# A graph layer's node-side product kept as three bfloat16 parts, and a comparison's constants kept in the PSUM bank of the counts

## The chip, the core and the metric

The kernel runs on one core of a Trainium2 chip. The metric is the device time of one execution in microseconds (us). Before the change, ten runs gave a median of 2495.02 us (2490.36 to 2504.91). The core has five engines that each work through a queue of their own in order: PE (TensorE, matrix products into PSUM; PEld is its load of the stationary operand), DVE (VectorE), ACT (ScalarE), POOL (GpSimd, which here issues the scattering transfers) and SP (SyncE, which here issues the other transfers). PSUM is the memory that PE writes its results to; it is divided into banks of 2 KB in each of 128 partitions.

## The reference

A layer of a graph network over N = 12,500 nodes of 64 features and E = 212,500 edges (`src`, `dst`, one weight each), sorted by `dst`:

```python
h = jnp.maximum(_layernorm(x, axis=-1), 0.0)
edge_in = jnp.concatenate([h[row], h[col], dist], axis=1)      # row = src, col = dst
e = jax.nn.silu(edge_in @ eW1 + eb1)
e = jax.nn.silu(e @ eW2 + eb2)
agg = jax.ops.segment_sum(e, row, num_segments=h.shape[0])
node_in = jnp.concatenate([h, agg], axis=1)
out = jax.nn.silu(node_in @ nW1 + nb1) @ nW2 + nb2
x = x + out
```

All numbers are float32. Since `edge_in @ eW1` is a sum over its parts, it can be formed as A[src] + B[dst] + dist * w + eb1, with A = h @ eW1[:64] and B = h @ eW1[64:128] computed once for each node.

## The kernel before

**Two tables.** `products` (line 668) computes, for four of the hundred "buckets" of 125 nodes at a time, A into the DRAM table `ta` and B into `tb` (256 KB stores from SP, lines 678 and 683); it runs 25 times. It is a generator: each `yield` is a place at which other work is put between its steps. `turns` (line 687) keeps up to three of these generators going at once, and the iterator `feed` hands out their steps, four or three to a piece of the work below, later two to a hook.

**Sending the edges.** The edges come in 208 blocks of 1024 in order of `dst`. For each block, `count` (line 344) finds for every edge its place in the bucket of its `src`. On DVE it compares the block's bucket numbers `bkE` with the row 1 to 100 of `nodes1` (lines 354 to 359; 128x800 results `oh` in bfloat16), reduces `oh` to counts `each` (line 362), and later multiplies `oh` with the running counts `full` (line 402), reduces that to `rank` (line 404) and makes the row numbers `to` (line 406). The running counts lie in PSUM: PE adds `before` times `each` to them (line 388) and, at the start of the next block's turn, `rest` times `each` (line 347). `send` (line 412) forms B[dst] + dist * w + eb1 for the block's edges with eight matrix products (line 427), copies them to SBUF on ACT (lines 437 and 443), and POOL scatters the rows to the DRAM array `q` in eight indirect transfers for each block (line 450; 1661 in all). The tile `to` has four buffers (line 268), so the `to` of one block waits until the scatters of the block four back have landed. Each block's turn is cut in three pieces (`PIECES`, line 486).

**Working off the rows.** The rows of `q` are taken in twelve levels (`LEVELS`, line 56) of 25 batches of four buckets. Levels 0, 1 and 8 to 11 have one row of 128 slots for each bucket (one step to a batch), levels 2 to 7 have two (two steps to a batch); there are 450 steps of four 128-row tiles. A level is fetched when all blocks that can write to it have been sent. `fetch` (line 492) loads a batch of `q` rows (`qt`) and the four buckets' rows of `ta` (`a`) four batches ahead. A step then is:

- `s_lr`, line 526: PE spreads each row's node number (bfloat16) over 125 partitions;
- `s_one_t`, line 531: DVE compares it, giving the one-hot matrix `oneT`;
- `s_pt`, lines 540 and 546: PE transposes the four tiles into `pt`, and adds `a` times `oneT`, which gives each row its A[src]; one product of 128 columns for each of four tiles where a batch has one step, one of 256 columns for each of two buckets where it has two; then ACT applies SiLU (line 550);
- `s_bias`, `s_p2`, lines 572 to 582: the second layer, float32;
- `s_one`, `s_seg`, `s_add`, lines 559, 592 and 603: another one-hot matrix, and the sums for each node, added to `aggT` on DVE.

In the last level each batch ends with the node layer (`nodes`, line 239). The queues of PE, DVE, ACT and SP are written out in the order of the program: the table `turn` (line 610) lists the parts of a step with the steps they run ahead, and each `None` in it is a hook at which pieces of the sending are put in, at a rate (`marks`) that finishes a level's blocks before that level's first fetch. If a check of the lists' assumptions fails, `general_sums` (line 950) computes all of it in another way; the profile has no instruction of it.

Of the kernel before, what the change touches and what calls it, by code (L numbers as in the profile page):

```python
# [38 lines left out]
P = 128  # L39
L = 125  # L40
# [8 lines left out]
TB = BLK // P  # L49
PAIR = 2 * BLK  # L50
BEYOND = 20
G = 4
# [21 lines left out]
def tile_gnn(ctx: ExitStack, tc: tile.TileContext, x, src, dst, ew, eW1, eb1, eW2, eb2, nW1, nb1, nW2, nb2, out):  # L74
# [111 lines left out]
    bad = const.tile([P, 2], F32, name="bad")  # L186
    nc.vector.memset(bad, 0.0)

    ta = dram.tile([P * NB, H], F32, name="ta")
    tb = dram.tile([P * NB, H], F32, name="tb")  # L190
    dests = dram.tile([NP, NQR, 2, QR], BF16, name="dests")

# [76 lines left out]
    with ExitStack() as work:  # L269
# [5 lines left out]
                engines={mybir.EngineType.PE, mybir.EngineType.DVE, mybir.EngineType.Activation, mybir.EngineType.SP}  # L275
            )
        )
        full = sgp.tile([P, NB], F32, name="full")
        nc.tensor.matmul(full, before, identb[:, :NB], start=True, stop=True)
        nc.vector.memset(full, -1.0)  # L280
        mine = cnt.tile([P, TB, NB], F32, name="mine")
        sums = []
        blk, lists = {}, {}
# [60 lines left out]
        def count(s):  # L344

            if s > 0:
                nc.tensor.matmul(full, rest, sums.pop(), start=False, stop=True, skip_group_check=True)
            if s < nblocks:
                bc, win, pick = blk[s]
                p, g = s // 2, s % 2  # L350
                whole = p > 0 and (2 * p + 2) * BLK <= E
                buckets = bkE[:, g * TB : (g + 1) * TB, p]
                oh = wk.tile([P, TB, NB], BF16, name="oh")
                nc.vector.tensor_tensor(  # L354
                    oh,
                    nodes1[:, None, :NB].to_broadcast([P, TB, NB]),
                    buckets[:, :, None].to_broadcast([P, TB, NB]),
                    op=OP.is_equal,
                )
                each = wk.tile([P, NB], BF16, name="each")  # L360
                with nc.allow_low_precision("whole numbers up to eight"):
                    nc.vector.tensor_reduce(each, oh.rearrange("p t b -> p b t"), AX.X, OP.add)  # L362
                sums.append(each)
            limits = [(SURE[w], OP.is_gt) for w in ready_at if s == ready_at[w]]
            closed = s > 0 and (s == nblocks or needed[s] != needed[s - 1])
            if closed:
                limits.append((SURE[needed[s - 1]], OP.is_lt))
            if s == nblocks:
                limits.append((ROWS, OP.is_gt))
            if limits:  # L370
                u = wk.tile([P, NB], F32, name="u")
                v = wk.tile([P, 1], F32, name="v")
            for limit, op in limits:
                nc.vector.tensor_scalar(u, full, float(G * limit - 1), None, op0=op)
                nc.vector.tensor_reduce(v, u, AX.X, OP.max)
                nc.vector.tensor_tensor(bad[:, 1:2], bad[:, 1:2], v, op=OP.add)
            if s == nblocks:
                return
            if closed and LEVELS[needed[s - 1]][2]:
                nc.vector.tensor_scalar(full, full, float(G * ENDS[needed[s - 1]] - 1), None, op0=OP.max)  # L380
            if not whole:
                nc.vector.tensor_scalar(pick, bc, same, plus, op0=OP.is_equal, op1=OP.add)
            elif g == 0:
                nc.vector.tensor_scalar(lists[p][1], lists[p][0], same, plus, op0=OP.is_equal, op1=OP.add)
            yield
            if g == 0 or not whole:
                weights(s)
            nc.tensor.matmul(full, before, each, start=False, stop=True, skip_group_check=True)  # L388
            if g == 0:
                assert p in scaled  # L390
                both = bkE[:, :, p].rearrange("p (g t) -> p g t", g=2)
                wide = [P, 2, TB, TB]
                eq = wk.tile(wide, F32, name="eq")
                nc.vector.tensor_tensor(
                    eq, both[:, :, :, None].to_broadcast(wide), both[:, :, None, :].to_broadcast(wide), op=OP.is_equal
                )
                nc.vector.tensor_tensor(eq, eq, early[:, None].to_broadcast(wide), op=OP.mult)
                pre = wk.tile([P, 2 * TB], F32, name="pre")
                nc.vector.tensor_reduce(pre.rearrange("p (g t) -> p g t", g=2), eq, AX.X, OP.add)
                nc.vector.tensor_tensor(offE[:, :, p], offE[:, :, p], pre, op=OP.add)  # L400
            yield
            nc.vector.tensor_tensor(mine, oh, full[:, None, :].to_broadcast([P, TB, NB]), op=OP.mult)  # L402
# [3 lines left out]
            nc.vector.scalar_tensor_tensor(  # L406
                to, rank, float(G * ROWS - 1), offE[:, g * TB : (g + 1) * TB, p], op0=OP.min, op1=OP.add
            )
            blk[s].append(to)
            yield  # L410
# [81 lines left out]
        def fetch(i):  # L492
            if i >= len(batches):
                return
            c, B, n = batches[i]
            assert not any(pending[: c + 1])
            while B not in done_a:
                next(feed)
            at = B * G * ROWS + G * (ENDS[c] - n * P)
            qt = ld2.tile([P, G * most, W], F32, name="qt")  # L500
            ins = nc.sync.dma_start(
                qt[:, : G * n, :].rearrange("p j w -> p (j w)"),
                q[at : at + G * n * P, :].rearrange("(p j) w -> p (j w)", p=P),
            ).ins
            for later in range(c + 1, len(LEVELS)):
                tc.declare_no_dep(ins, group=f"rows{later}", reason="these ranks were full before")
            tc.add_manual_dep(ins, last_rows[LEVELS[c][1] - 1].name, AFTER)
            tc.add_to_no_dep_group("loads", ins)
            a = ld2.tile([P, G, H], F32, name="a")
            nc.sync.dma_start(a, ta_buckets[:, B * G : B * G + G])  # L510
            batch[c, B] = [qt, a, None]
            if c == len(LEVELS) - 1:
                node_in[B] = nodes_in(B, ndp[0])
# [13 lines left out]
            st[k] = {"lr": lr}  # L527

        def s_one_t(k):
            oneT = wk.tile([L, G, P], F32, name="oneT")  # L530
            nc.vector.tensor_scalar(oneT, st[k].pop("lr")[:L], part1[:L, :], None, op0=OP.is_equal)  # L531
            st[k]["oneT"] = oneT

        def s_pt(k):

            (qt, a, _), tiles = of(k)
            oneT = st[k].pop("oneT")
            pt = mm.tile([P, G, P], F32, name="pt", tag="mm")
            for t, (j, _) in enumerate(tiles):
                nc.tensor.matmul(  # L540
                    pt[:, t, :], qt[:, j, :H], ident, is_transpose=True, start=t == 0, stop=False, skip_group_check=True
                )
            for b, same in itertools.groupby(range(G), lambda t: tiles[t][1]):
                same = list(same)
                cols = slice(same[0], same[-1] + 1)
                nc.tensor.matmul(  # L546
                    pt[:, cols, :], a[:L, b, :], oneT[:, cols, :], start=False, stop=True, skip_group_check=True
                )
            e1 = wk.tile([P, G, P], F32, name="e1")
            nc.scalar.activation(e1, pt, AF.Silu)  # L550
            st[k]["e1"] = e1
# [116 lines left out]
        def products(b0, g, xs):  # L668
# [5 lines left out]
            rows_a = fp.tile([P, G, H], F32, name="rows_a")  # L674
            product(0, hr, mm, "mm", rows_a)
            nc.sync.dma_start(hd[:, b // 2 : (b + G) // 2, :], hr)
            yield
            nc.sync.dma_start(ta_buckets[:, b : b + G, :], rows_a)
            done_a.append(b // G)
            got = fp.tile([P, G, H], F32, name="got")  # L680
            product(1, hr, mm, "mm", got)
            yield
            nc.sync.dma_start(tb_buckets[:, b : b + G, :], got)
            done_b.append(b // G)
            yield

        def turns(todo, width):
# [262 lines left out]
def general_sums(tc, N, E, NB, H, src, dst, ew, ta, tb, aggT, w1d, eb1b, w2, ident, ones, eb2r, part):  # L950
# [6 lines left out]
    with ExitStack() as ctx:  # L957
# [17 lines left out]
        def tile_of(at, n):  # L975
# [8 lines left out]
            nc.vector.tensor_scalar(pre[:n], w1d[:n], w[:n], None, op0=OP.mult)  # L984
            nc.vector.tensor_tensor(pre[:n], pre[:n], eb1b[:n], op=OP.add)
            for k, (idx, table) in enumerate(((si, ta[:]), (di, tb[:]))):
                got = gw.tile([P, H], F32, name=f"got{k}")
                nc.gpsimd.indirect_dma_start(
                    out=got[:n],
                    out_offset=None,  # L990
                    in_=table,
                    in_offset=bass.IndirectOffsetOnAxis(ap=idx[:n, :], axis=0),
                )
                nc.vector.tensor_tensor(pre[:n], pre[:n], got[:n], op=OP.add)
# [76 lines left out]
```

## Time and profile before

| | before |
|---|---|
| median of ten runs | 2495.02 us (2490.36 to 2504.91) |
| the profiled execution | 2492.33 us |
| its span, first to last instruction | 2490.5 us |
| PE busy | 2080.1 us (84%) |
| DVE busy | 1934.3 us (78%) |
| POOL busy | 1739.3 us (70%) |
| ACT busy | 1088.0 us (44%) |
| transfers | 443.83 MB, mean 178 GB/s |
| mean granted clock of PE | 0.924 of full speed |

The shares are means over stages with different limits. Steps begin at 252 us; before that PE, DVE and ACT work on the tables and the first blocks. POOL's scatters run from the first blocks to 2287 us. The last 200 us hold steps and node layers only. In an instruction row, "out<-in" names the tiles, "xN" the number of instructions; a float32 product shows as two PE instructions, and "mean ns of one" is the time from its start to its modelled end, which overlaps with the next one's.

### The profile page before, as it was taken

Reading aid. Unit: us, or ns where it says so; the run is one execution under the profiler, and the core shown is the slowest. Engines: PE = TensorE matmul, PEld = TensorE weight load, DVE = VectorE, ACT = ScalarE, POOL = GpSimd, SP = SyncE. Lnnn points to the kernel's source line nnn. Section 1 sums busy time; section 2 is a strip of 40 time slices with the busy share of each in tenths; the row PEclk is TensorE's granted clock in tenths of the full one; section 3 lists DMA queues with packets and bytes.
Section 4 is the critical chain, followed back from the end, with each engine's and each line's share of the span. In section 5 each row is a group of like instructions: output and inputs, shape, how many; then the busy total and the mean of one; then the engine's idle time right before and its main releaser. Section 6 shows DMA issues by size and latency. Waiting matters only on the chain.

```text
span 2490.5 us, 46228 instructions
## 1 busy us (share of the span) xinstructions
PE 2080.1 (84%) x16191; PEld 1846.1 (74%) x16191; DVE 1934.3 (78%) x3005; ACT 1088.0 (44%) x2403; POOL 1739.3 (70%) x1712
## 2 busy tenths in 40 slices
PE   3673687655788898898998888999999999999997
PEld 2452675544677787787888777888888889999986
DVE  7885677666787888888888887888889989986432
ACT  2442333222344454444444444455455555555442
POOL 4777777777777777777777777777777777762110
PEclk9965887777899999999999999999999999999999
DMA  4563556555566765666644454455455556665652
GB/s 116 185 211 118 171 182 190 169 172 174 180 220 204 231 203 170 220 221 207 207 161 160 160 164 150 165 174 173 163 164 178 179 164 201 212 210 180 189 162 66
DMA packets 237005, 443.83 MB, mean 178 GB/s; under 512 B 49804, under 2 KB 108735, under 8 KB 236561
## 3 DMA queue, kind: packets, MB, share of 16 engines
q1 hardware_dynamic: 158629, 269.79, 34.4%
q0 software_dynamic: 53536, 123.03, 14.2%
q10 hardware_dynamic: 24602, 47.98, 6.6%
q8 instruction: 131, 2.15, 0.4%
q14 instruction: 107, 0.88, 0.1%
HBM read 251.07 MB, written 189.55 MB: 177 GB/s over the span
## 4 chain that ended last, share of the span: by engine, by line
PE 33%; DVE 17%; DMA 16%; POOL 15%; issue 8%; ACT 2%; DVEq 0%; POOLq 0%; SPq 0%; ACTq 0%
DMA q<-qs,to 16%; POOL q L450 15%; PE seg L592 7%; PE pt L546 7%; PE p L578 6%; PE qp L427 5%; PE pt L540 4%; DVE each L362 3%; DVE oh L354 3%; DVE oneT L531 3%; DVE one L559 2%; PE lr L526 2%; DVE aggT L603 2%; DVE rank L404 1%; DVE mine L402 1%
## 5 line engine op out<-in xcount | busy, mean ns | idle before, releaser
L450 POOL DMA_INDIRECT q<-qs,to x1661 | 1710.1, 1030 | 584.1 <-issue 396.5
L550 ACT ACTIVATE e<-pt 128x512 f32<-128x512 f32 x450 | 268.8, 597 | 725.2 <-PE pt L546 691.0
L592 PE MATMUL seg<-one,e 128*128 128x125 f32 x3600 | 501.7, 284 | 75.2 <-DVE aggT L603 54.5
L592 PEld LDWEIGHTS seg<-one,e 128*128 128x128 f32 x3600 | 451.8, 197 | 99.8 <-issue 55.7
L578 PEld LDWEIGHTS p<-w,e 128*128 128x128 f32 x3600 | 472.5, 198 | 43.8 <-issue 27.1
L578 PE MATMUL p<-w,e 128*128 128x128 f32 x3600 | 501.7, 284 | 0.0
L546 PE MATMUL pt<-oneT,a 125*128 125x128 f32 (+1 forms) x2400 | 486.4, 337 | 11.7 <-DVE oneT L531 11.7
L437 ACT COPY qs<-qp 128x512 f32<-128x512 f32 x416 | 223.2, 589 | 544.0 <-PE qp L427 508.1
L427 PEld LDWEIGHTS qp<-win,pick 64*128 64x128 f32 x1662 | 177.4, 216 | 290.9 <-issue 228.7
L546 PEld LDWEIGHTS pt<-oneT,a 125*128 125x128 f32 x2400 | 366.6, 200 | 31.3 <-DVE oneT L531 14.0
L531 DVE TENSOR_SCALAR oneT<-lr,part 125x512 f32<-125x512 f32 x450 | 335.1, 745 | 53.5 <-PE lr L526 50.6
L362 DVE TENSOR_REDUCE each<-oh 128x100 bf16<-128x800 bf16 x208 | 315.3, 1516 | 7.2
L559 DVE TENSOR_TENSOR one<-nodes,qt 128x500 f32<-128x500 f32 x450 | 301.7, 670 | 0.0
L427 PE MATMUL qp<-win,pick 64*128 64x256 f32 x1662 | 287.3, 463 | 5.5 <-DMA win<-tb 5.0
L540 PE MATMUL pt<-ident,qt 128*128 128x128 f32 x1800 | 289.3, 285 | 0.8 <-DVE oneT L531 0.8
L582 ACT ACTIVATE e<-p 128x512 f32<-128x512 f32 x450 | 269.2, 598 | 7.9 <-PE p L578 7.8
L572 ACT COPY p<-b2f 128x512 f32<-128x512 f32 x450 | 267.2, 594 | 0.4 <-DMA qt<-q 0.4
L406 DVE SCALAR_TENSOR_TENSOR to<-rank,offE 128x8 int32<-128x8 f32 x208 | 36.2, 174 | 287.9 <-DMA q<-qs,to 283.2
L603 DVE TENSOR_TENSOR aggT<-aggT,seg 128x500 f32<-128x500 f32 x275 | 184.0, 669 | 71.3 <-PE seg L592 70.6
L388 PE MATMUL full<-each,before 128*128 128x100 bf16 x208 | 45.0, 216 | 227.4 <-DVE each L362 208.3
L540 PEld LDWEIGHTS pt<-ident,qt 128*128 128x128 f32 x1800 | 199.8, 147 | 20.1 <-issue 17.2
L404 DVE TENSOR_REDUCE rank<-mine 128x8 f32<-128x800 f32 x208 | 205.0, 986 | 7.2
(144 smaller groups left out, 1617.0 us busy)
## 6 DMA issues: line engine op xcount, KB each, us to landing
qt<-q SPq DMA_DIRECT2D x150, 576.0 KB
a<-ta SPq DMA_DIRECT2D x300, 256.0 KB
qt<-q SPq DMA_DIRECT2D x150, 288.0 KB
q<-zeros ACTq DMA_DIRECT2D x25, 1080.0 KB
q<-qs,to POOLq DMA_INDIRECT x1661
q<-zeros ACTq DMA_DIRECT2D x10, 1440.0 KB
bc<-dests SPq DMA_DIRECT2D x103, 128.0 KB
win<-tb SPq DMA_DIRECT2D x416, 30.0 KB
```

Of the source, the lines that this page charges most:

```text
L362: nc.vector.tensor_reduce(each, oh.rearrange("p t b -> p b t"), AX.X, OP.add)
L427: nc.tensor.matmul(qps[i][:, t, : n_of[t]], pick[at, t * P : (t + 1) * P], win[at, : n_of[t]], start=True, stop=True)
L450: ins = nc.gpsimd.indirect_dma_start(out=q[:], out_offset=bass.IndirectOffsetOnAxis(ap=to[:k, j : j + 1], axis=0), in_=qs[:k, t, a, :], in ...
L531: nc.vector.tensor_scalar(oneT, st[k].pop("lr")[:L], part1[:L, :], None, op0=OP.is_equal)
L540: nc.tensor.matmul(pt[:, t, :], qt[:, j, :H], ident, is_transpose=True, start=t == 0, stop=False, skip_group_check=True)
L546: nc.tensor.matmul(pt[:, cols, :], a[:L, b, :], oneT[:, cols, :], start=False, stop=True, skip_group_check=True)
L550: nc.scalar.activation(e1, pt, AF.Silu)
L559: nc.vector.tensor_tensor(one.rearrange("p (b j) l -> p b j l", j=n), nodes1[:, None, None, :].to_broadcast(wide), loc[:, tiles[0][1] : ti ...
L572: nc.scalar.copy(p2, b2f)
L578: nc.tensor.matmul(p2[:, t, :], e1[:, t, :], w2, start=False, stop=t == G - 1, skip_group_check=True)
L582: nc.scalar.activation(e2, p2, AF.Silu)
L592: nc.tensor.matmul(item[2][:, b, :], e2[:, t, :], one[:, t, :], start=j < G, stop=j >= G * (n - 1))
```

## The change

Two things. First, `ta` holds A as three bfloat16 numbers whose sum is A (768 bytes for each node where it was 512): the value rounded, the rest rounded, and what is left. `products` makes them with two copies on ACT and two subtractions on DVE for each group, takes six yields where it took four, and stores `ta` after `tb`. `oneT` becomes bfloat16, and line 546 issues three bfloat16 products where it issued one of float32, all added to `pt`. `a` is loaded with 384 KB for each batch where it was 256 KB. Second, the tile of the counts becomes 200 columns wide: `full` is its first half, and the second half, `numbers`, is set once to the numbers 1 to 100. Line 354 reads `numbers` there, in PSUM, where it read `nodes1` in SBUF. `numbers` and `full` lie in one tile and one bank.

```diff
--- before.py
+++ after.py
@@ -186,7 +186,7 @@
     bad = const.tile([P, 2], F32, name="bad")
     nc.vector.memset(bad, 0.0)
 
-    ta = dram.tile([P * NB, H], F32, name="ta")
+    ta = dram.tile([P * NB, 3 * H], BF16, name="ta")
     tb = dram.tile([P * NB, H], F32, name="tb")
     dests = dram.tile([NP, NQR, 2, QR], BF16, name="dests")
 
@@ -275,9 +275,11 @@
                 engines={mybir.EngineType.PE, mybir.EngineType.DVE, mybir.EngineType.Activation, mybir.EngineType.SP}
             )
         )
-        full = sgp.tile([P, NB], F32, name="full")
+        counts = sgp.tile([P, 2 * NB], F32, name="counts")
+        full, numbers = counts[:, :NB], counts[:, NB:]
         nc.tensor.matmul(full, before, identb[:, :NB], start=True, stop=True)
         nc.vector.memset(full, -1.0)
+        nc.vector.tensor_copy(numbers, nodes1[:, :NB])
         mine = cnt.tile([P, TB, NB], F32, name="mine")
         sums = []
         blk, lists = {}, {}
@@ -353,7 +355,7 @@
                 oh = wk.tile([P, TB, NB], BF16, name="oh")
                 nc.vector.tensor_tensor(
                     oh,
-                    nodes1[:, None, :NB].to_broadcast([P, TB, NB]),
+                    numbers[:, None, :].to_broadcast([P, TB, NB]),
                     buckets[:, :, None].to_broadcast([P, TB, NB]),
                     op=OP.is_equal,
                 )
@@ -506,8 +508,8 @@
                 tc.declare_no_dep(ins, group=f"rows{later}", reason="these ranks were full before")
             tc.add_manual_dep(ins, last_rows[LEVELS[c][1] - 1].name, AFTER)
             tc.add_to_no_dep_group("loads", ins)
-            a = ld2.tile([P, G, H], F32, name="a")
-            nc.sync.dma_start(a, ta_buckets[:, B * G : B * G + G])
+            a = ld2.tile([P, G, 3, H], BF16, name="a")
+            nc.sync.dma_start(a.rearrange("l b s f -> l b (s f)"), ta_buckets[:, B * G : B * G + G])
             batch[c, B] = [qt, a, None]
             if c == len(LEVELS) - 1:
                 node_in[B] = nodes_in(B, ndp[0])
@@ -527,7 +529,7 @@
             st[k] = {"lr": lr}
 
         def s_one_t(k):
-            oneT = wk.tile([L, G, P], F32, name="oneT")
+            oneT = wk.tile([L, G, P], BF16, name="oneT")
             nc.vector.tensor_scalar(oneT, st[k].pop("lr")[:L], part1[:L, :], None, op0=OP.is_equal)
             st[k]["oneT"] = oneT
 
@@ -543,9 +545,10 @@
             for b, same in itertools.groupby(range(G), lambda t: tiles[t][1]):
                 same = list(same)
                 cols = slice(same[0], same[-1] + 1)
-                nc.tensor.matmul(
-                    pt[:, cols, :], a[:L, b, :], oneT[:, cols, :], start=False, stop=True, skip_group_check=True
-                )
+                for i in range(3):
+                    nc.tensor.matmul(
+                        pt[:, cols, :], a[:L, b, i, :], oneT[:, cols, :], start=False, stop=i == 2, skip_group_check=True
+                    )
             e1 = wk.tile([P, G, P], F32, name="e1")
             nc.scalar.activation(e1, pt, AF.Silu)
             st[k]["e1"] = e1
@@ -674,14 +677,21 @@
             rows_a = fp.tile([P, G, H], F32, name="rows_a")
             product(0, hr, mm, "mm", rows_a)
             nc.sync.dma_start(hd[:, b // 2 : (b + G) // 2, :], hr)
-            yield
-            nc.sync.dma_start(ta_buckets[:, b : b + G, :], rows_a)
-            done_a.append(b // G)
+            parts = fp.tile([P, G, 3, H], BF16, name="parts")
+            nc.scalar.copy(parts[:, :, 0, :], rows_a)
+            yield
+            nc.vector.tensor_tensor(rows_a, rows_a, parts[:, :, 0, :], op=OP.subtract)
             got = fp.tile([P, G, H], F32, name="got")
             product(1, hr, mm, "mm", got)
             yield
             nc.sync.dma_start(tb_buckets[:, b : b + G, :], got)
             done_b.append(b // G)
+            nc.scalar.copy(parts[:, :, 1, :], rows_a)
+            yield
+            nc.vector.tensor_tensor(parts[:, :, 2, :], rows_a, parts[:, :, 1, :], op=OP.subtract)
+            yield
+            nc.sync.dma_start(ta_buckets[:, b : b + G, :], parts.rearrange("p b s f -> p b (s f)"))
+            done_a.append(b // G)
             yield
 
         def turns(todo, width):
@@ -984,14 +994,20 @@
             for k, (idx, table) in enumerate(((si, ta[:]), (di, tb[:]))):
-                got = gw.tile([P, H], F32, name=f"got{k}")
+                got = gw.tile([P, H], F32, name="got1") if k else gw.tile([P, 3, H], BF16, name="got0")
...
```

More of the change, by code (lines that the diff above doesn't have):

```diff
@@ L986, in tile_of @@
             for k, (idx, table) in enumerate(((si, ta[:]), (di, tb[:]))):
-                got = gw.tile([P, H], F32, name=f"got{k}")
+                got = gw.tile([P, H], F32, name="got1") if k else gw.tile([P, 3, H], BF16, name="got0")
                 nc.gpsimd.indirect_dma_start(
-                    out=got[:n],
+                    out=got[:n] if k else got[:n].rearrange("p s f -> p (s f)"),
                     out_offset=None,
@@ L993, in tile_of @@
                 )
-                nc.vector.tensor_tensor(pre[:n], pre[:n], got[:n], op=OP.add)
+                if k:
+                    nc.vector.tensor_tensor(pre[:n], pre[:n], got[:n], op=OP.add)
+                    continue
+                v = gw.tile([P, H], F32, name="v0")
+                nc.vector.tensor_tensor(v[:n], got[:n, 0], got[:n, 1], op=OP.add)
+                nc.vector.tensor_tensor(v[:n], v[:n], got[:n, 2], op=OP.add)
+                nc.vector.tensor_tensor(pre[:n], pre[:n], v[:n], op=OP.add)
             sf = gw.tile([P, 1], F32, name="gsf")
```

## The prediction

> **What bounds the kernel now.** I read the slices first, then the waits, the scatters beside DVE in order of time, and PE's order of time near the end.
>
> ```profile
> PE   3673687655788898898998888999999999999997
> POOL 4777777777777777777777777777777777762110
> PEclk9965887777899999999999999999999999999999
> L450 POOL DMA_INDIRECT q<-qs,to x1661 | 1710.1, 1030 | 584.1 <-issue 396.5
> ```
>
> POOL is 7 tenths busy in every slice until 2200 us, while PE and DVE vary. A scatter takes 1.03 us and nearly all the idle before scatters is a fixed 0.30 us. So POOL is full although its share says 70%, and the waits say who stands behind it:
>
> ```profile
> POOL q L450 <- ACT qs L443: 83.1, 35, 23.0
> DVE to L406 <- DMA q<-qs,to: 283.2, 97, 7.0
> ```
>
> POOL waited for its data 83 us in all: 23 in one wait at the start, 51.6 after 2210 us. Between them it starves for less than 10 us. DVE instead waits 283 us for scatters to land. So POOL sets the pace until those DVE waits end, about 2015 us (22.5 us of them in 1700 to 2210, one of 3.6 in 2000 to 2100). From 2015 to 2235 PE is busy 213.9 of 220 us, and the backlog of scatters drains; from 2300 to 2400 PE is busy 100.0 of 100. The path is POOL to 2015 us, PE after that.
>
> Next, why a scatter takes 1.03 us on average, when most take 0.97:
>
> ```profile
> 1509.59 0.98 DVE L402 TENSOR_TENSOR mine<-oh,full 128x800 f32<-128x800 bf16 x1
> 1510.03 0.97 POOL L450 DMA_INDIRECT q<-qs,to  x1 [0.30 <-issue]
> ...
> 1516.68 0.67 DVE L559 TENSOR_TENSOR one<-nodes,qt 128x500 f32<-128x500 f32 x1
> 1516.74 1.44 POOL L450 DMA_INDIRECT q<-qs,to  x1 [0.30 <-DMA q<-qs,to]
> ...
> 1524.73 0.98 DVE L354 TENSOR_TENSOR oh<-nodes,bkE 128x800 bf16<-128x800 f32 x1
> 1524.86 1.70 POOL L450 DMA_INDIRECT q<-qs,to  x1 [0.30 <-ACT e L550]
> ```
>
> A scatter that starts inside line 354 or line 559 (both inputs in SBUF) is stretched until 0.8 us after that DVE instruction ends: 1525.71 to 1526.56 and 1517.35 to 1518.18. One that starts inside line 402, which reads `full` in PSUM, is not. I went through all 1661 scatters in this way: 99.7 us lie above 0.975 us each. By the DVE instruction that ends about 0.15 us into the held scatter's last 0.97, 47.7 us belong to line 354 (114 scatters; 45.7 us before 2015), 35.0 to line 559 (118), 5.6 to line 394, at most 0.1 to line 402.
>
> **The change part by part.** The sum is made against the profiled execution, 2492.33 us (span 2490.5), which is 2.7 us below the median of 2495.02.
>
> *Line 354 reads PSUM.* Its own time stays: 985 ns now, 979 for line 402, which reads PSUM in the same pattern. Its holds on POOL go: between 0 and 47.7 us; I take the 45.7 before 2015, where POOL is the path, because line 402 is the nearest row and holds nothing.
> The Trainium skill, "SBUF — State Buffer", section "Who interferes with whom", says that a two-input DVE instruction takes only the read side of the port shared with GpSimd, and infers that making transfer descriptors there needs the write side, so that such an instruction would not stall transfers. By that this term would be 0 and the sum 2487 us; the trace's 1.70 us beside 0.97 disagrees.
>
> *The new wait.* `numbers` shares tile and bank with `full`, which PE writes at line 347 just before line 354 is issued. If accesses are ordered by bank and not by columns, line 354 must wait for that product, and with it everything behind it on DVE: line 362, the `pick` of line 384, then the next `oneT`, for which PE's line 546 waits; line 388 waits for line 362. In the trace of before, which lacks this wait, I compared each line 347's end with line 354's start: 95 of 207 products end later, by 81.8 us in all, 67.8 of them before 2015 and 14.0 after; the largest past 700 us is 1.85. Ends: 0 and 81.8. I take the wait as there. Before 2015 it is covered by the 283 us that DVE spends waiting for scatters, and costs 0; without that cover, 67.8. After 2015 DVE is busy 200.3 of 220 us and PE takes `each` soon, so 9 of the 14.0 us.
>
> *Line 546.* The prices stand in order of time on PE:
>
> ```profile
> 2351.49 0.39 PE L526 MATMUL lr<-identb,qt 128*125 128x128 bf16 x4
> 2351.72 0.61 PE L540 MATMUL pt<-ident,qt 128*128 128x128 f32 x4
> 2352.16 1.06 PE L546 MATMUL pt<-oneT,a 125*128 125x128 f32 x8
> 2353.05 1.01 PE L246 MATMUL z<-aggT,w1g 128*128 128x250 f32 x4
> ```
>
> From start to next start, line 526 takes 0.23 us for four bfloat16 products with four new stationary operands: 0.0575 each. Line 546 takes 0.89 for four float32 products (eight instructions). Twelve bfloat16 products at 0.0575 make 0.69: 0.20 less; the single starts are 0.055 to 0.06 apart, for loads too, so I take 0.22 at most and 0.21 as the price. A two-bucket step had 0.87 us (1511.62 to 1512.49) and gets six products of 256 columns, twice 0.0575 each, 0.69: 0.18 less. Until 2015 PE isn't the path and the gain is idle time. After it, 106 steps remain (56 to 2235, 50 later), all of one bucket a tile: 11.8 and 10.5 us. Ends: 0, and 106 times 0.22 or 23.
> The Trainium skill, "TensorE: Matmul & The Clock Gate", section "Back-to-back issue gap", gives about 81 ns for a sustained pair of load and 128-column product. Twelve would be 0.97 us, 0.08 more than now, and the sum some 31 us higher; line 526's row, four pairs in 0.23 us, says less, though it is a run of only four.
>
> *`oneT` in bfloat16:* 0. Line 354 writes bfloat16 at the price at which line 402 writes float32, and line 531 reads PSUM as before.
>
> *Three parts in `products`.* ACT gets 50 copies of 128x512 at 0.59 us (line 572's row), 30 us beside an ACT that is 53% busy in 100 to 200 us. DVE gets 50 subtractions of 128x512 at 0.69 (line 559's 0.67 for 500 columns), 34 us, in some 60 to 270 us. There DVE's idle time is 55.8 us in 100 to 300, 42.7 of it waiting for scatters, and POOL has up to three blocks (some 31 us) queued. So the work is covered; if that cover is gone it is 34 us. Each subtraction waits for a copy, and ACT itself stands up to 11 us behind PE there, so I leave 4 us. The subtractions read SBUF twice and hold POOL like line 559: 35.0/450, or 0.08 us each, 4 us; were every one caught by line 559's longest, 0.5 us, 25. The 50 additional turns of `feed` at three a piece end it some 17 pieces (about 58 us) later, still before the steps' fifth fetch. On SP the `ta` store moves behind `tb` and waits for DVE; `pick`, `bc` and `win` loads stand behind it. SP lost 21.0 and 15.1 us to its waits at lines 676 and 678; POOL's queue covers that too: 0, or about 15 without it. The single copy to `numbers` is 0.2 us.
>
> *`a` loads.* 300 times 128 KB more, 38 MB on 443.83, beside transfers 0.56 busy. At 178 GB/s a load is 0.7 us longer; four batches of lead (13 us and more) hide it: 0. Without that lead it would be 106 times 0.7, 74 us, after 2015.
>
> Sum: -45.7 (holds) + 4 (new holds) + 4 (early) + 9 (wait late) - 11.8 - 10.5 = -51. 2492.3 - 51 = 2441, and beside the median of the runs 2444. I say 2442.
>
> **The rivals.** *No new wait, or a free one:* ordering goes by columns. Then the 9 us fall away and the early cost too: 2492.3 - 45.7 + 4 - 23 = 2428. For it: line 347 ends before line 354 starts in 112 of 207 blocks.
> *PE or DVE takes the path early:* DVE with its new wait and PE at 96% in 1700 to 2015 leave POOL's faster pace unused after about 1500 us. The holds gained until then are some three quarters, 34 us, and if the last stage's gain is given back as waits, 2492.3 - 34 + 8 = 2466, up to 2480. For it: DVE waited for scatters only 22.5 us after 1700. Against it: PE's work falls by about 0.2 of some 4.4 us a step, more than POOL's pace rises (0.028 of 1.306 us).
> *Slower:* at line 354 the new wait turns counting into an alternation of PE and DVE, and `to` comes too late for POOL. DVE's reserve is 283/208 = 1.36 us a block. If each block waited the 1.85 us that is the longest now, POOL would idle 0.49 us in 189 blocks, 93 us, and the gain of 51 is gone: 2534. It decides from 1.36 + 51/189 = 1.63 us a block; the mean lateness now is 0.39, which speaks against it.
> *Holds stay:* reading PSUM doesn't free POOL. Then 2492.3 + 8 + 9 - 22 = 2487. Line 402 speaks against it.
>
> **How the numbers follow.** The forecast has 0.54, no wait 0.13, an early change of the path 0.14, holds stay 0.05, slower 0.14. The forecast's own range is 2428 to 2456. The whole range, 2422 to 2478, takes in the second case, all gains of 47.7 and 23, and the third; it leaves out the slow case and most of the holds case, and some of the tails. Within 0.2% (5 us) is about what a measurement of this kernel can't tell from no change. Faster: 0.54 + 0.13 + 0.13 of the early change and 0.02 of the holds case, 0.82; within: 0.04; slower: 0.14.
>
> **What would show it.** Scatters near 1.00 us mean, none stretched by line 354; a wait of line 354 for line 347 of 50 to 100 us in all; DVE's wait for scatters less than 283; line 546 near 0.69 us from start to next start; the last step near 5.7 us where it is 5.9 (2351.49 to 2357.38). I am wrong if POOL shows waits for `qs` in mid-run, if line 354 waits above 1.6 us a block, or if twelve products take 0.89 us or more.

## The result and the profile after

The changed kernel takes 2475.96 us (median of 8 runs, 2472.95 to 2479.28) against 2495.93 us for the kernel before (28 runs): a ratio of 0.9917, 95% interval 0.9905 to 0.9928. It is faster by 20 us where 53 were forecast. The profiled execution took 2480.67 us (span 2478.8), 4.7 us above its median, while the one of before lay 3.6 us below; so the two traces show 11.7 of the 20 us, and a difference of a few us between two traces is used below only where several runs agree in it.

From the page of the changed kernel: two rows of slices, and two groups of instructions (busy time, mean ns of one, idle time before them and what ended it). Line numbers have moved: 450 is now 452, 354 is 356, 347 is 349, 546 is 549, 559 is 562, 603 is 606.

```profile
PE   3465686555688889888889888898999999989997
POOL 4677777777777777777777777777777777762210
L452 POOL DMA_INDIRECT q<-qs,to x1661 | 1682.6, 1013 | 603.7 <-issue 400.6
L356 DVE TENSOR_TENSOR oh<-counts,bkE 128x800 bf16<-128x800 f32 x208 | 204.8, 985 | 65.2 <-PE counts L349 62.8
```

POOL is still full until about 2180 us. A scatter takes 1.013 us on average; it was 1.030 before, and would be 1.00 if line 354's holds had gone and nothing else had changed (1.030 - 47.7/1661). Line 356 costs what it did, 985 ns, but now DVE stands idle ahead of it.

From the waits of the changed kernel (total us, times, longest):

```profile
DVE to L408 <- DMA q<-qs,to: 161.8, 61, 7.2
DVE oh L356 <- PE counts L349: 62.8, 57, 5.4
PE seg L595 <- DVE aggT L606: 79.5, 41, 5.7
```

The comparison's wait for the counts' product is there, 62.8 us of it. DVE's reserve, its waiting for scatters, has shrunk from 283.2 to 161.8 us. PE waits longer for the additions of `aggT` (54.5 before), but that total doesn't measure the new wait: it is 85.3 us in e3 below, where line 356 reads SBUF again, and 81.5 in e1, where most of the new wait is gone.

In order of time, two places of the changed kernel; first the stage after 2015 us:

```profile
2186.11 0.67 DVE L562 TENSOR_TENSOR one<-nodes,qt 128x500 f32<-128x500 f32 x1
2186.47 1.16 POOL L452 DMA_INDIRECT q<-qs,to  x1 [0.30 <-issue]
...
2194.49 0.21 PE L349 MATMUL counts<-each,rest 128*128 128x100 bf16 x1
...
2194.73 0.99 DVE L356 TENSOR_TENSOR oh<-counts,bkE 128x800 bf16<-128x800 f32 x1 [1.11 <-PE counts L349]
2194.77 0.97 POOL L452 DMA_INDIRECT q<-qs,to  x1 [0.30 <-issue]
...
2195.76 1.53 DVE L364 TENSOR_REDUCE each<-oh 128x100 bf16<-128x800 bf16 x1
...
2197.20 0.57 DVE L386 TENSOR_SCALAR pick<-bc,same,plus 128x512 f32<-128x512 bf16 x1
...
2197.68 0.66 DVE L606 TENSOR_TENSOR aggT<-aggT,seg 128x500 f32<-128x500 f32 x1
...
2198.49 1.13 PE L595 MATMUL seg<-one,e 128*128 128x125 f32 x8 [1.73 <-DVE aggT L606]
```

A scatter that starts inside line 356 takes 0.97 us: no hold. One that starts inside line 562 is still held (1.16). The rest shows what the wait does when PE is the path. Line 356 loses 1.11 us to line 349; the three instructions behind it are late, the third of them is the addition that frees the only `seg` buffer, and PE stands 1.73 us ahead of its next sums.

Then the last steps, on PE:

```profile
2342.99 0.39 PE L528 MATMUL lr<-identb,qt 128*125 128x128 bf16 x4
2343.22 0.61 PE L542 MATMUL pt<-ident,qt 128*128 128x128 f32 x4
2343.66 0.83 PE L549 MATMUL pt<-oneT,a 125*128 125x128 bf16 x12
2344.34 1.06 PE L246 MATMUL z<-aggT,w1g 128*128 128x250 f32 x4
2345.33 0.69 PE L249 MATMUL z<-hrn,w1n 64*128 64x250 f32 x4
```

The twelve products take 0.68 us from start to next start (median of all such steps 0.67); line 546's eight instructions took 0.89. The next group took 0.95 us before (2353.05 to 2354.00) and takes 0.99 now.

### The profile page after: what moved, and what is told of

It is laid out like the page before. It is cut to its first block, busy times and chain, and to the rows that moved or that the text cites. A ratio compares the mean times of both kernels' runs of the same rounds, so it can differ in the third digit from the quotient of the medians.

```text
span 2478.8 us, 48612 instructions
## 1 busy us (share of the span) xinstructions
PE 2005.7 (81%) x17391; PEld 1776.1 (72%) x17391; DVE 1972.3 (80%) x3056; ACT 1114.7 (45%) x2453; POOL 1712.3 (69%) x1712
## 4 chain that ended last, share of the span: by engine, by line
PE 32%; DVE 29%; DMA 16%; POOL 11%; issue 9%; ACT 3%; DVEq 0%; SPq 0%; ACTq 0%; POOLq 0%
DMA q<-qs,to 13%; POOL q L452 11%; PE seg L595 7%; PE p L581 6%; DVE each L364 5%; PE qp L429 5%; DVE oh L356 5%; PE pt L549 5%; PE pt L542 3%; DVE oneT L533 3%; DVE one L562 3%; DVE aggT L606 2%; DVE rank L406 2%; DVE mine L404 2%; PE lr L528 2%
## 5 line engine op out<-in xcount | busy, mean ns | idle before, releaser
L452 POOL DMA_INDIRECT q<-qs,to x1661 | 1682.6, 1013 | 603.7 <-issue 400.6
L581 PEld LDWEIGHTS p<-w,e 128*128 128x128 f32 x3600 | 453.4, 198 | 29.1 <-issue 25.3
L549 PE MATMUL pt<-oneT,a 125*128 125x128 bf16 (+1 forms) x3600 | 388.6, 253 | 5.0 <-DVE oneT L533 5.0
L533 DVE TENSOR_SCALAR oneT<-lr,part 125x512 bf16<-125x512 f32 x450 | 335.0, 744 | 59.5 <-PE lr L528 58.6
L549 PEld LDWEIGHTS <-a 125*128 125x128 bf16 x3600 | 301.8, 101 | 30.5 <-issue 6.1
L356 DVE TENSOR_TENSOR oh<-counts,bkE 128x800 bf16<-128x800 f32 x208 | 204.8, 985 | 65.2 <-PE counts L349 62.8
L390 PE MATMUL counts<-each,before 128*128 128x100 bf16 x208 | 44.9, 216 | 252.2 <-DVE each L364 228.5
```

Source lines behind the costliest of these rows:

```text
L356: nc.vector.tensor_tensor(oh, numbers[:, None, :].to_broadcast([P, TB, NB]), buckets[:, :, None].to_broadcast([P, TB, NB]), op=OP.is_equal,)
L452: ins = nc.gpsimd.indirect_dma_start(out=q[:], out_offset=bass.IndirectOffsetOnAxis(ap=to[:k, j : j + 1], axis=0), in_=qs[:k, t, a, :], in ...
L549: nc.tensor.matmul(pt[:, cols, :], a[:L, b, i, :], oneT[:, cols, :], start=False, stop=i == 2, skip_group_check=True)
L581: nc.tensor.matmul(p2[:, t, :], e1[:, t, :], w2, start=False, stop=t == G - 1, skip_group_check=True)
```

## The experiments

The ratios, which are what is compared between runs, are to runs of the kernel before made beside each: their median was 2499.38 us beside e1 to e4, 2496.59 beside e5 to e8 and 2497.30 beside e9 to e12. Each profile is one execution; that of e3 is 7.2 us faster than its median, that of e8 5.3 us slower, and the others lie within 5 us of theirs.

I counted every scatter's stretch above 0.975 us, and put it down to the DVE instruction that ends about 0.15 us into its last 0.97. From here on, lines are numbered in the text as in the kernel before, unless it is said otherwise. "Scatter 1440" and the steps are counted from 0, a step is timed by the start of its SiLU (line 550), and "long gaps" are what the gaps above 0.35 us between scatters have over the usual 0.30 us; scatter 1440 started at 1965.8 us before, close to where POOL ceased to be the path. The sum of the last two columns is the span.

| run | ratio to before (95% interval) | stretch in all, us | by line 354 | by line 559 | by line 394 | scatter 1440 starts, us | from there to the end, us |
|---|---|---|---|---|---|---|---|
| before | 1 | 99.7 | 47.7 | 35.0 | 5.6 | 1965.8 | 524.7 |
| the change | 0.9917 (0.9905 to 0.9928) | 74.7 | 0 | 45.9 | 12.7 | 1956.5 | 522.3 |
| e1 the change, late `rest` | 0.9869 (0.9853 to 0.9886) | 72.0 | 0 | 46.6 | 8.8 | 1946.2 | 514.3 |
| e2 numbers only | 0.9946 (0.9929 to 0.9963) | 59.7 | 0 | 39.8 | 7.2 | 1940.1 | 539.6 |
| e3 parts only | 0.9977 (0.9962 to 0.9991) | 104.7 | 41.3 | 40.2 | 7.7 | 1968.3 | 514.3 |
| e4 numbers, late `rest` | 0.9885 (0.9862 to 0.9907) | 69.5 | 0 | 41.3 | 13.6 | 1942.6 | 526.7 |
| e5 as e1, line 559 in PSUM too | 0.9765 (0.9735 to 0.9795) | 18.9 | 0 | 0 | 3.2 | 1899.8 | 533.1 |
| e6 as e1, four turns a piece | 0.9905 (0.9873 to 0.9936) | 71.2 | 0 | 46.5 | 8.2 | 1952.9 | 517.0 |
| e7 as e1, without two levels' additions | 0.9851 (0.9820 to 0.9882) | 69.7 | 0 | 44.1 | 9.1 | 1948.3 | 507.5 |
| e8 as e4, without two levels' additions | 0.9818 (0.9787 to 0.9848) | 64.5 | 0 | 45.5 | 7.9 | 1937.1 | 519.4 |
| e9 as e5, two turns a piece | 0.9758 (0.9729 to 0.9788) | 20.2 | 0 | 0 | 3.0 | 1899.9 | 531.5 |
| e10 as e4, line 559 instead of 354 | 0.9915 (0.9886 to 0.9945) | 65.6 | 52.6 | 0 | under 1.3 | 1941.5 | 530.4 |
| e11 as e5, without parts | 0.9770 (0.9742 to 0.9799) | 19.4 | 0 | 0 | 4.6 | 1896.6 | 544.2 |
| e12 as e4, loads of 384 KB | 0.9883 (0.9854 to 0.9912) | 69.7 | 0 | 46.3 | 11.8 | 1939.2 | 530.5 |

### The change taken apart (e1 to e4)

Two theories stood against each other. W: the comparison's new wait ate the gain of PE's stage. H: the holds that line 354 gave up were taken over by the two-input comparisons that are left. They don't exclude each other. The wait can be taken away without a race, by issuing the product of `rest` later; `numbers` and the comparison stay where they are:

```diff
-            if s > 0:
-                nc.tensor.matmul(full, rest, sums.pop(), start=False, stop=True, skip_group_check=True)
+            checked = bool(limits) or closed
+            if s > 0 and checked:
+                add_rest()
...
+            if s > 0 and not checked:
+                add_rest()
             nc.tensor.matmul(full, before, each, start=False, stop=True, skip_group_check=True)
```

e1 is the changed kernel with this edit.

> The changed kernel, with the product of `rest` issued directly ahead of the product of `before` instead of ahead of the comparison (except in the blocks whose counts are checked), so that the comparison has no product to wait for that was issued just before it. Theory W (the comparison's new wait took back the gain of the last stage): the waits of the comparison for the counts' products fall from 62.8 us to under 15, and the time from 2476 to 2460 to 2468. Theory H (the wait was covered; the holds on POOL that line 354 gave up were taken over by the other two-input comparisons): the waits vanish too, but the time stays within 4 us of 2476, and the stretch of scatters stays near 75 us in all.

e2 is the kernel before with the tile `counts` and line 354 reading `numbers`, and nothing else.

> The kernel before with only the numbers moved to PSUM. The terms of the prediction: -45.7 of holds and +9 of the wait give 2458. Theory H: the holds of line 354 go, but those of the one-hot comparison rise from 35 to 44 us or more and those of the equality of line 394 from 6 to 12, so that the stretch is 65 to 72 us instead of 100, and the time is 2478 to 2488. Theory W: the gain in POOL's stage is lost in the stage after 2015 us, so that the time is 2488 to 2495.

e3 is the changed kernel with that one operand put back:

```diff
-                    numbers[:, None, :].to_broadcast([P, TB, NB]),
+                    nodes1[:, None, :NB].to_broadcast([P, TB, NB]),
```

> The changed kernel with the comparison reading the numbers in SBUF again. If the parts pay only in PE's last stage (22 us by the prediction) and cost 8 us early: 2478 to 2484, with the step after 2235 us shorter by 0.2 us and the scatters up to 300 us later by 6 to 8 us. If the parts also lengthen the time in which POOL sets the pace (more transfers, more holds by the subtractions): 2486 to 2495. The stretch of scatters is 100 to 106 us.

e4 is e2 with the later product of `rest`.

> The kernel before with the numbers in PSUM and the product of `rest` issued directly ahead of that of `before`. Theory W: 10 us or more below the run with the numbers alone, 2470 to 2480. Theory H: within 4 us of the run with the numbers alone.

Measured medians: e1 2464.98, e2 2483.86, e3 2491.71, e4 2471.63 us, beside 2499.38 for the kernel before on that chip. The first line below is from the waits of e2, the other three from those of e1, where line 360 is the comparison (354 before), 368 the reduction to `each` (362), 350 the product of `rest` (347) and 394 the product of `before` (388):

```profile
DVE oh L356 <- PE counts L349: 79.1, 77, 4.9
```

```profile
DVE oh L360 <- PE counts L350: 6.6, 7, 1.6
PE counts L350 <- DVE oh L360: 102.8, 48, 6.9
PE counts L394 <- DVE each L368: 119.6, 113, 6.0
```

With the later product the comparison's wait falls from 62.8 to 6.6 us. PE now waits for the comparison ahead of the product of `rest`, but it waited at that place for `each` anyway: 228.5 us in all before this edit, 102.8 + 119.6 with it. The time falls by 0.0048 of 2496, 12 us, with the parts, and by 0.0061, 15 us, without them. Theory W holds. Where the loss was: from step 340 to step 400 (1999.2 to 2236.8 us before) the kernel with the numbers alone takes 8.3 us longer than before, and with the later product 0.1 us less; the changed kernel 2.5 us longer, and with the later product 4.7 less. PE's wait in these steps for the addition that frees `seg` goes the same way. The lines are from the waits of the kernel before (1999.2 to 2236.8 us), of the changed kernel (1992.2 to 2232.3) and of e1 (1980.6 to 2213.6):

```profile
PE seg L592 <- DVE aggT L603: 4.8, 5, 2.1
PE seg L595 <- DVE aggT L606: 13.7, 9, 2.3
PE seg L599 <- DVE aggT L610: 7.3, 7, 2.3
```

It is 11.2 us in e2, which has the new wait, and 5.0 in e3 and in e4, which have none or little of it. A part of the loss lies at the start: the long gaps between scatters up to scatter 1440 are 5.4 us before, 10.8 with the numbers alone and 6.8 with the later product; 16.1 in the changed kernel and 9.3 with it. (Between the traces of the changed kernel and e1 lie 18.3 us, more than the 12 between the medians.)

Theory H holds as well, in the stretch: line 354's 47.7 us are gone in e1, e2 and e4, but line 559's 35.0 have become 40 to 47 and line 394's 5.6 have become 7 to 14, so that the stretch falls by 28 to 40 us and not by 47.7 (by 25 in the changed kernel, whose subtractions add 5.1). The time of e2 was the one that H gave, but its holds rose less than expected (39.8 and 7.2, not 44 and 12). And the size of the rise is uncertain: e3, where line 354 still reads SBUF, has 40.2 us of holds by line 559, as many as e2, and 41.3 by line 354. The eight kernels of the table that move line 354 alone have 39.8 to 46.6 by line 559. The parts alone are worth 0.0023, or 6 us; 2491.71 us is the second of e3's two cases (2486 to 2495), not the first (2478 to 2484). In its trace they start the end stage later (1968.3) but make it 10.4 us shorter. The two halves of the change add up: 0.0054 (e2) and 0.0023 (e3) make 0.0077, where the whole took off 0.0083.

### The holds (e5, e10)

If a hold that is taken away is partly taken over by others, the mirror image should show it: line 559 moved to PSUM, line 354 left in SBUF. And with both in PSUM nearly all of the stretch should go. The edit widens `counts` to 225 columns and changes line 559's operand:

```diff
-                nodes1[:, None, None, :].to_broadcast(wide),
+                numbers[:, None, None, :].to_broadcast(wide),
```

> The run with the late product of `rest`, and the second one-hot comparison of each step reads its numbers in the PSUM bank of the counts too (125 of them). Theory H (a hold that is taken away is partly taken over by the comparisons that are left): the stretch of scatters falls from 72 to 25 to 35 us, no longer to 20 or less, as line 394's equality and the table's subtractions take some; scatter 1440 starts 25 to 40 us earlier than with the late product alone, if POOL still sets the pace there. The rival, that the new waits on the bank (of the comparison for the counts' products, and of these for the comparison) cost more than the holds: the DVE waits for the counts' products rise above 60 us and the time is 2465 or more. My forecast is 2445 to 2460.

> The kernel before with the late product of `rest`, where only the step's one-hot comparison (line 559) reads its numbers in PSUM, and the block's comparison (line 354) reads SBUF as before. Theory H, the mirror image: the holds of line 559 (35 us) go and those of line 354 rise from 47.7 to 53 to 60 us, since each is then caught with the share of a random start (65% of 208, 0.4 us each); the stretch is 65 to 75 us, and the time 2470 to 2485. The rival, that the two kinds of hold are independent: line 354 stays at 45 to 50 us.

The group of the scatters on the page of e10, then on the page of e5, and two of e5's waits (line 456 is the scatter, 412 makes `to`, 566 is the one-hot comparison of a step, 350 the product of `rest`):

```profile
L456 POOL DMA_INDIRECT q<-qs,to x1661 | 1673.0, 1007 | 602.6 <-issue 405.0
```

```profile
L456 POOL DMA_INDIRECT q<-qs,to x1661 | 1625.0, 978 | 615.6 <-issue 400.1
```

```profile
DVE to L412 <- DMA q<-qs,to: 87.9, 32, 6.4
PE counts L350 <- DVE one L566: 128.4, 79, 7.0
```

e10: 2474.94 us, and line 354's holds rise from 47.7 to 52.6 us, just under what was expected (53 to 60) and above the rival's 45 to 50. Counted between 300 and 2015 us, it catches a scatter in 107 of 163 blocks, 66%, the share of a random start, where it was 93 of 161 (58%) with line 559's holds beside it. e5: 2438.70 us, 0.9765 of before, the fastest kernel so far; the scatter is down to 0.978 us, and scatter 1440 starts 46 us earlier than in e1 (25 to 40 were expected), and the time is below the forecast of 2445 to 2460. The expectation of 25 to 35 us of stretch missed too, 18.9 is left: line 394 did not take over, its holds fell to 3.2 us. So there is no fixed sum of holds that must fall on somebody.

The trace of before shows how. Between 300 and 2015 us, the one-hot comparison (line 559) that follows a line 354 with a hold catches a scatter in 16 of 93 cases, the one that follows a line 354 without a hold in 19 of 68; for the second one after it, it is 17 of 93 and 25 of 68. The trace of e3, counted in the same way with scatters above 1.00 us, agrees: 13 of 80 and 24 of 82, then 19 of 80 and 39 of 82. A hold fixes when the next scatters start relative to DVE's order, and that start is one at which line 559 mostly misses. With line 354 out of the way, line 559 caught 155 of 342 (45%) in the changed kernel where it had been 86 of 337 (26%).

The Trainium skill, "SBUF — State Buffer", section "Who interferes with whom", infers that two-input DVE instructions would not stall the making of descriptors on GpSimd; it also says that one with two SBUF inputs contends with a GpSimd instruction that reads SBUF. Here moving one input of each of two such comparisons took 53 us of stretch (72.0 to 18.9) out of the scatters and 26 us off the time; on the inference the measurement decides. What a scatter's issue reads or writes in SBUF while it is held, these runs don't show.

### The early loss (e6, e9)

In the changed kernel scatter 160 starts 8 us later than before. Either the tables end late, because their generators need 50 more turns, or the added work itself is in the way. e6 hands out four turns for each piece instead of three in e1, e9 two in e5:

```diff
             next(pieces)
-            for _ in range(3):
+            for _ in range(4):
                 next(feed, None)
```

> The run with the late product of `rest`, with four turns of the tables' generators for each piece of the sending where there were three, so that the 50 additional turns no longer end the tables later. If the early loss (scatter 160 starts 4 us later than before there, 8 us in the changed kernel) comes from the tables ending late: scatter 160 is 3 to 4 us earlier, and the time 2461 to 2463. If it comes from the added DVE and ACT work itself, which is then packed denser: scatter 160 is as late or later, and the time 2465 to 2470.

> The run with both comparisons reading PSUM, with two turns of the tables' generators for each piece of the sending where there were three. If the tables' added work starves POOL early when it is packed densely (four turns lost 8 us): the long gaps between scatters up to 300 us fall below 6 us, and the time is 2432 to 2438. If two turns only move the work to where the steps have begun: 2437 to 2446.

e6 took 2472.71 us, 0.9905 against 0.9869: denser is worse, the long gaps up to scatter 1440 rise from 9.3 to 16.9 us. e9 took 2434.49 us (0.9758), which can't be told from e5 (0.9765); its gaps are 9.6 against 8.9. Scatter 160 starts 3.6 us earlier in e9 than in e5 (263.0 against 266.6), but scatter 1440 at the same time. So it is the work, not the lateness of the tables, but thinning it out gains nothing that can be measured. From the waits of the changed kernel up to 300 us:

```profile
DVE rows_a L683 <- ACT parts L681: 15.9, 8, 4.2
DVE parts L691 <- ACT parts L689: 8.2, 5, 2.9
```

DVE stands 24 us behind ACT's copies there, in a stage in which it had 43 us of reserve.

### What held the parts' gain back (e7, e8, e11, e12)

From step 340 to 400 the parts won 4.6 us (e1 against e4), where 0.21 us a step would be 12.6. Theory D has it that DVE held the stage back, rival T that the larger loads of `a` did. e7 and e8 leave out the additions of levels 8 and 9 on DVE, in e1 and in e4, so that their part of the result is missing:

```diff
-            else:
+            elif c not in (8, 9):
                 nc.vector.tensor_tensor(v, v, seg, op=OP.add)
```

> The run with the late product of `rest`, without the additions of two levels' sums (levels 8 and 9, 50 steps between about 2015 and 2235 us, 0.67 us of DVE each; their part of the result is left out). Theory D (in that stage DVE, 90% busy, ate the gain of line 546: 3.6 us were gained in 55 steps where 12 were forecast): against the same run without the parts, the steps 345 to 400 now gain 8 to 12 us, and the time is 2452 to 2458. Rival T (the larger loads of `a` slow that stage): the gain of the parts in these steps stays 2 to 5 us.

> The same additions left out of the run that has the numbers in PSUM and the late product of `rest`, but no parts. Theory D: PE sets the pace there without the parts, so that the time falls by 0 to 5 us only, 2467 to 2472, against 7 to 13 us with the parts. Rival T: both fall by the same, within 3 us.

e12 gives e4 the transfers of the changed kernel: rows of 192 float32 in `ta`, of which 128 are used, and 64 zeros written by DVE for each.

```diff
-    ta = dram.tile([P * NB, H], F32, name="ta")
+    ta = dram.tile([P * NB, 3 * H // 2], F32, name="ta")
...
-            a = ld2.tile([P, G, H], F32, name="a")
+            a = ld2.tile([P, G, 3 * H // 2], F32, name="a")
```

> The kernel before with the numbers in PSUM and the late product of `rest` (2472), with rows of 768 bytes in `ta` as in the changed kernel (the last 256 zero and unused), so that it makes the transfers of the changed kernel without its products. Rival T (the larger loads eat the gain): 5 to 10 us slower, 2477 to 2482, the loss in the steps 340 to 400. Otherwise within 3 us of 2472.

e12 took 2467.73 us, 0.9883 against e4's 0.9885: 43 MB more of transfers (486.4 against 443.8) cost nothing that shows, as the prediction had it. The intervals alone leave some 9 us open, but the steps 340 to 400, where rival T had its loss of 5 to 10 us, took 1.8 us longer than in e4's trace. In the traces of e7 and e8 steps 340 to 400 got shorter by 9.9 us with the parts (14.6 against e1's 4.7) and by 7.1 without (7.2 against 0.1), so that the parts' gain there rose only from 4.6 to 7.4 us, not to 8 to 12. The medians don't bear theory D out either: 2459.55 for e7 (0.9851 against 0.9869) and 2453.02 for e8 (0.9818 against 0.9885), so without the parts the time fell by more. What is shown is that PE, 95 to 97% busy there, did not hold that stage alone: without 34 us of additions it got 7 to 10 us shorter, with and without the parts. The edit takes away two things at once, DVE's time and PE's wait for the addition that frees `seg` (7.3 us in e1 and 5.0 in e4, 0.6 in e7 and none in e8), and these runs don't separate them. Of the 12.6 us, PE's busy time in these steps shows 8.5 (230.3 us in e4, 221.8 in e1); its idle time grew from 7.2 to 11.2 us. Why stays open.

e11 is e5 without the parts.

> The kernel before with both comparisons reading PSUM and the late product of `rest`, without the parts. With POOL faster, PE and DVE set the pace over a longer stretch. If the parts are worth 0.22 us of PE in each step there, this is 12 to 25 us slower than with the parts (2439): 2451 to 2464. If DVE or the loads hold that stretch, the parts are worth 8 us or less: 2435 to 2447.

It took 2439.72 us, 0.9770 against 0.9765: with both comparisons in PSUM, the parts are worth nothing that these runs can tell from zero (the intervals leave some 10 us open), though PE is busy 1990.5 us with them and 2049.6 us without. The first expectation, 12 to 25 us, fell. In the two traces the parts start the end stage 3.2 us later and make it 11.1 us shorter; the medians lie 1 us apart.

## Why the prediction was right or wrong

The direction, the path (POOL to about 2015 us, PE after it) and the mechanism of the holds were right, and the time lies inside the range, near its end. The size was wrong: 20 us instead of 53. In the two traces:

- **The holds, -45.7 and +4 for new ones: mis-sized, the largest error.** Line 354's holds did go, all 47.7 us. But the step took the holds of line 559 (35.0) and line 394 (5.6) as fixed; they became 45.9 and 12.7. (Of line 559's rise some 5 us may be the spread between traces: e3 has 40.2 with line 354 in place.) The subtractions' 5.1 were priced about right. Up to scatter 1440 the stretch above 0.975 us fell from 84.9 to 66.3: 18.6 us, where the two terms make 41.7.
- **The early loss, +4: too small.** The long gaps between scatters grew by 10.7 us (5.4 to 16.1). "POOL's queue covers that" failed: DVE's subtractions stood behind ACT, and the wait for the counts' product came on top; e2 and e3 put 5.4 us of gaps on the wait alone and 3.7 on the parts alone. Scatter 1440 so started 9.3 us earlier, not 38.
- **The new wait, 0 before 2015 and +9 after it: there, as taken, and too cheap.** It is 62.8 us where 81.8 were the lateness in the trace of before. Taking it out won 12 us (15 without the parts), some of it before 2015, where it was put at nothing. The step followed the wait to line 388 and `oneT`, and missed the addition to `aggT` behind it, which frees PE's only `seg` buffer: PE's wait for it in steps 340 to 400 rose from 4.8 to 13.7 us, and is 7.3 in e1.
- **Line 546, -11.8 and -10.5: the price right, the yield half.** Twelve products take 0.67 us; 0.69 was forecast. But the group behind them takes 0.04 us longer, so a last step went from 5.89 to 5.73 us (2342.04 to 2347.77, both starts of line 595 of the changed kernel), not 5.7 exactly as 0.21 would have it, and steps 400 to 449 won 7.2 us. From 340 to 400, PE was not the only thing in the way: with the wait the changed kernel lost 2.5 us there, without it it won 4.7.
- **At nothing, and rightly:** the output type of `oneT` (744 ns, 745 before), line 354's own time, and the larger loads as far as e12 can tell.

Together: 9.3 us to scatter 1440 and 2.4 after it make the 11.7 us between the traces, where 38 and 13 were forecast. Of the rivals, "PE or DVE takes the path early" comes nearest by its time, but not by its mechanism: POOL's pace was used all the way (between scatters 160 and 1440 the changed kernel has about 3 us of long gaps), it had just not become as fast. The slower rival did not come: the mean wait was 62.8/208 = 0.30 us a block, far below 1.63.

The Trainium skill, "TensorE: Matmul & The Clock Gate", section "Back-to-back issue gap", would have given 0.97 us for twelve pairs, an estimate from its 81 ns a pair. The run of twelve takes 0.67, or 56 ns each, so the row of four was the better guide.

## What to carry to other kernels

In these runs the stalls that one engine inflicts on another are not a sum of separate prices: each stall sets the start of what follows and so shields later ones; price a stall that is taken away together with what the remaining ones would catch at a random start (line 559 caught 33 to 45% between 300 and 2015 us in the four kernels that had moved line 354 alone, against 26% before and 32% in e3). A constant put beside numbers that PE writes, here in one tile and one PSUM bank (these runs don't tell which of the two orders the accesses), buys a wait with PE's order, and the price is read from what stands behind the waiting instruction, down to the one that frees a buffer; issuing the write of that bank where a write is waited for anyway (e1) took nearly all of the wait away at no cost that shows. The best kernel of these runs, with both comparisons in PSUM and the late product (e5 or e9, 0.976 of before), keeps the second half of the change; without the parts (e11, 0.977) it can't be told from it.

## What the runs showed that I had not expected

A scatter is held by a DVE instruction with two SBUF inputs only if it starts inside it, and then until about 0.8 us after its end; one that begins 0.1 us or more after the scatter's start leaves it alone: of 345 scatters of the kernel before beside which line 354 or 559 began that late, with none of the comparisons at their start, 327 took at most 1.00 us. With no such instruction left but short ones the mean scatter is 0.978 us, beside an undisturbed 0.97. And two comparisons moved to PSUM together took more out of the scatters than the sum of each alone: the stretch fell by 80.3 us (e11), against 30.2 (e4) and 34.1 (e10), which is what the taking over would make of it. In the times this can't be told: the ratio fell by 0.0230, against 0.0115 and 0.0085, and the difference of 0.0030 lies within the intervals.
